# A two-layer graph attention kernel: nodes taken in 25 groups that fit 17 slots of edges, in place of blocks of 128 nodes with 18 slots

## The chip, the cores and the metric

The kernel runs on one core of a Trainium2 chip. The metric is the device time of one execution in microseconds (us). Engines are named as in the profile: PE is TensorE's matmul and PEld its weight load, DVE is VectorE, ACT is ScalarE, POOL is GpSimd and SP is SyncE.

## The reference

There are 3125 nodes with 768 features each, and 53125 edges that are sorted by destination. An edge has a source, a destination and one of three types. Two relational graph attention layers run one after the other (four heads in the first, one in the second); then the input is added and each row is normalized.

```python
def rgat_conv(x, W, q, k, b, src, dst, etype, heads, out_ch, n_nodes):
    xr = jnp.einsum('nd,rdf->rnf', x, W)
    oi = xr[etype, dst]
    oj = xr[etype, src]
    alpha = jax.nn.leaky_relu(oi @ q + oj @ k, NEG_SLOPE)
    m = jax.ops.segment_max(alpha, dst, num_segments=n_nodes)
    e = jnp.exp(alpha - m[dst])
    z = jax.ops.segment_sum(e, dst, num_segments=n_nodes)
    a = e / (z[dst] + EPS)
    msg = (a[:, :, None] * oj.reshape(-1, heads, out_ch)).reshape(-1, heads * out_ch)
    return jax.ops.segment_sum(msg, dst, num_segments=n_nodes) + b

h = jax.nn.elu(rgat_conv(x, W1, q1, k1, b1, src, dst, edge_type, 4, 192, n))
x = _layernorm(x + rgat_conv(h, W2, q2, k2, b2, src, dst, edge_type, 1, 768, n), axis=-1)
```

The number of edges that end in a node is not constant: it is drawn, 17 on average.

## The kernel before

Edges are handled in **slots** of 128, one edge to a partition. Nodes are handled in 25 **blocks** of 128 (the last has 53). The edges of a block lie in one run of the sorted list, whose start is counted on the chip and read by SP into a register. A block always takes `SL = 18` slots, 2304 edges, from its start on; the last block takes `SLL = 9`. Edges behind the block's own are in the window too, and `a_index2` gives them an index out of bounds, so that the gather leaves them out. All in all there are `NK = 24 * 18 + 9 = 441` slots, and each slot is gone through three times. Were a block to have more edges than its slots hold, a flag would be set and a second, general kernel would run behind this one.

Every engine's instructions stand in an order that is written out by hand: each of the three phases has a table of events, `ev`, by step, and the recording loop goes through the steps.

- **The prelude** (`prepare`, `weights_kq`, `nodes_kq`) loads W and x, makes the small table of source scores `kt1` (four numbers for each node and type) and the destination scores `qq`, and writes four lists of edges to HBM (`ed_d`, `dr_d`). In `prepare` a loop of 26 DVE instructions (L205) counts the edges below each block's border; a matmul sums these counts over partitions into `starts`. The pieces of `prepare` are spread between the other work by `more(n)`.
- **Phase 1** (`phase1`) has 144 steps with one `d_group` each: 18 matmuls (L629) that make one half row block of the table `tab1`, the rows x W. `d_row` copies it out on ACT (L641) and SP stores it. Six steps make one block of nodes, and beside them the attention weights of one block are worked out: SP loads the lists (`a_load` L471, `a_load2` L477, `a_window` L511), `a_index` turns them on PE (L516), `a_index2` makes the indices, `a_gathers` gathers 18 x 128 source scores with one indirect DMA for each slot from POOL's queue (L451, `kt`), `a_q` to `a_q3` add the destination's score, `a_alpha` (L565) adds the two and is the instruction that waits for the gathers, and `a_max`, `a_scan`, `a_back`, `a_put` make the weights `pall`.
- **Phase 2** (`phase2`) gathers whole rows of `tab1`, 3088 bytes for each edge, again one indirect DMA for each slot (L451, `share`, nine buffers). ACT weighs them (`high`, L788), DVE makes the remainder (`low`, L802), POOL or DVE makes the selecting matrix (`sel`, L790: POOL for two slots of three) and four matmuls sum a slot into its node rows (`sums`, L821). The last block goes first (`order`), then blocks 0 to 23. When a block is summed, `e_y` to `e_s2` make its hidden rows, and 18 pieces of six matmuls (`d_part`, L876), one with each slot of the next block, make its rows of `tab2`; `d_row` (L884) copies them and SP stores them (L890).
- **Phase 3** (`phase3`) gathers rows of `tab2` in the same way (L451, `G`, a ring of 36 slots as six tiles of six). `a_alpha` (L1013) waits for all gathers of a block; `a_turn`, `a_scan` (with the list that L966 loads), `a_exp`, `a_back`, `a_put` make the weights, `high` and `low` the parts, `sums` (L1090) the sums. `LAG = SL + 11` steps lie between a slot's gather and its sum. `e_y` to `e_out` normalize a block and store it.

POOL's gathers of all phases stand in one queue, `gather_rows` is the helper that issues them, so all have the line L451 and are told apart by the tile they fill: `kt`, `share`, `G`.

Of the kernel before, what the change touches and what calls it, by code (L numbers as in the profile page):

```python
# [37 lines left out]
SL = 18  # L38
CAP = SL * P

SLL = 9

FRONT = 256
BACK = CAP + 256

PART = 6
# [5 lines left out]
def kernel(  # L52
# [8 lines left out]
):  # L61

# [26 lines left out]
    NK = (NB - 1) * SL + SLL  # L89
# [5 lines left out]
    first_rows = {0: 0, 1: 1, 2: 2, NB - 1: 3}  # L95
# [4 lines left out]
    tab2 = dram.tile([NP * R, RW], F32, name="ftab2")  # L100
    kt1 = dram.tile([NP * R, 4], F32, name="kt1")
    xb_d = dram.tile([NP, D], F32, name="xb_d")
# [11 lines left out]
    starts = keep.tile([1, 32], I32, name="starts")  # L114
# [3 lines left out]
    dl = keep.tile([P, NB, SL], F32, name="fdl")  # L118
    rel = keep.tile([P, NB, SL], F32, name="rel")
    pall = keep.tile([P, NB, SL, H1], F32, name="pall")  # L120
    q1s = keep.tile([P, NB, H1, R, 3], BF, name="q1s")
# [48 lines left out]
    def prepare(work, bank, wide, half):  # L170
# [7 lines left out]
        cnt = work.tile([EP, 32], F32, name="cnt")  # L178
        V.memset(cnt, 0.0)
# [20 lines left out]
        blk = tile_(I32)  # L200
        V.tensor_single_scalar(blk, di, 7, op=ALU.logical_shift_right)
        bb, junk, dr = (half[:EP, i * ET:(i + 1) * ET] for i in range(3))
        V.tensor_copy(bb, blk)
        for b in range(NB + 1):
            V.tensor_scalar(junk, bb, float(b), 0.0, op0=ALU.is_lt, op1=ALU.add, accum_out=cnt[:, b:b + 1])  # L205
            yield
            if b == 10:
                win = wide[:EP, :ET + P]
                c = ed_d[1:2, FRONT:FRONT + 1]
                G.dma_start(win, bass.AP(tensor=c.tensor, offset=c.offset, ap=[[ET, EP], [1, ET + P]]))  # L210
                rx = tile_(F32)
                V.scalar_tensor_tensor(rx, si, float(R), ti, op0=ALU.mult, op1=ALU.add)
                store(ed_d[0], rx)
                yield
                tf = tile_(F32)
                V.tensor_copy(tf, ti)
                store(ed_d[2], tf)
                yield
                V.tensor_single_scalar(di, di, P - 1, op=ALU.bitwise_and)
                V.tensor_copy(dr, di)  # L220
                store(dr_d[0], dr)
                yield
# [3 lines left out]
        V.tensor_reduce(cnt[:, 30:31], junk, AX.X, ALU.add)  # L226
        yield
        V.tensor_tensor(junk, dB, win[:, P:ET + P], op=ALU.is_equal)
        V.tensor_reduce(cnt[:, 31:32], junk, AX.X, ALU.add)
# [8 lines left out]
        T.matmul(pc[:1, :32], ones, cnt, start=True, stop=True)  # L238
        cf = work.tile([1, 32], F32, name="cf")
        V.tensor_copy(cf, pc[:1, :32])  # L240
        V.tensor_copy(starts, cf)
        yield
        big = work.tile([1, 32], F32, name="big")
        V.tensor_sub(big[:, :NB], cf[:, 1:NB + 1], cf[:, 0:NB])
        V.tensor_scalar(big[:, :NB - 1], big[:, :NB - 1], float(CAP), None, op0=ALU.is_gt)
        V.tensor_scalar(big[:, NB - 1:NB], big[:, NB - 1:NB], float(SLL * P), None, op0=ALU.is_gt)
        V.tensor_copy(big[:, 30:32], cf[:, 30:32])
        V.memset(big[:, NB:30], 0.0)
        tot = work.tile([1, 1], F32, name="tot")
        V.tensor_reduce(tot, big, AX.X, ALU.add)  # L250
        V.tensor_copy(flag, tot)
# [90 lines left out]
    def nodes_kq(buf, pre, work, psum, bank, wk, kqs, wH, wL, qq, more, edges_ready):  # L342
# [86 lines left out]
        for m in range(1, NCH + 2):  # L429
# [7 lines left out]
            more(3)  # L437
# [5 lines left out]
    ends = {min((b + 1) * SL, NK) - 1 for b in range(NB)}  # L443
# [10 lines left out]
    def start(b, into):  # L454
        if b not in into:
            into[b] = nc.sync.value_load(starts[0:1, b:b + 1], min_val=0, max_val=E)
        return into[b]

    def at(t, rw, off, ap, s):

        c = t[rw:rw + 1, bass.ds(s + (FRONT + off), 1)]
# [36 lines left out]
    def phase1(pre, work, psum, wH, wL, qq):  # L498
        kts = [work.tile([P, SL, H1], F32, name=f"kt{i}", bufs=1) for i in range(3)]
        als = [work.tile([P, SL + 2, H1], F32, name=f"al{i}", bufs=1) for i in range(2)]  # L500
        for t in als:
            V.memset(t, 0.0)
# [165 lines left out]
        def slots(b):  # L668
            return SLL if b == NB - 1 else SL

# [1073 lines left out]
```

## Time and profile before

| what | value |
|---|---|
| runs before | 2519.32 us median of 3 (2488.62, 2519.32, 2528.63) |
| profiled execution, its own time | 2285.11 us |
| its span, first to last instruction | 2283.3 us |
| mean granted TensorE clock in it | 0.950 |
| PE busy | 2049.8 us (90%), 11055 matmuls |
| DVE busy | 1555.7 us (68%) |
| ACT busy | 1401.7 us (61%) |
| POOL busy | 1733.3 us (76%), 1685 instructions |
| gathers of POOL | 3 x 441 |
| moved by DMA | 508.22 MB |

The profiled execution is one run with the profiler on. Busy times count what an engine executes, not the gaps in which it issues; a PE that is busy is not PE at its peak, since the ends of matmuls are modelled. [...]

### The profile page before, as it was taken

Reading aid. Unit: us, or ns where it says so; the run is one execution under the profiler, and the core shown is the slowest. Engines: PE = TensorE matmul, PEld = TensorE weight load, DVE = VectorE, ACT = ScalarE, POOL = GpSimd, SP = SyncE. Lnnn points to the kernel's source line nnn. Section 1 sums busy time; section 2 is a strip of 40 time slices with the busy share of each in tenths; the row PEclk is TensorE's granted clock in tenths of the full one; section 3 lists DMA queues with packets and bytes.
Section 4 is the critical chain, followed back from the end, with each engine's and each line's share of the span. In section 5 each row is a group of like instructions: output and inputs, shape, how many; then the busy total and the mean of one; then the engine's idle time right before and its main releaser. Section 6 shows DMA issues by size and latency. Waiting matters only on the chain.

```text
span 2283.3 us, 37563 instructions
## 1 busy us (share of the span) xinstructions
PE 2049.8 (90%) x11055; PEld 1765.0 (77%) x11055; DVE 1555.7 (68%) x4075; ACT 1401.7 (61%) x3197; POOL 1733.3 (76%) x1685
## 2 busy tenths in 40 slices
PE   6998988898886899999999999999489999899986
PEld 5888888888886799999999999999255555565554
DVE  7734434343432899999999999996266666676666
ACT  5411111111111788888888888885278888787885
POOL 4267777777776888888888888884677777777772
PEclk9989998999998899999999999999699999999998
DMA  6554544454455877777777777776788888888881
GB/s 181 178 149 164 170 145 145 161 170 145 159 184 158 308 245 234 233 230 235 234 235 237 228 233 240 236 233 219 256 283 298 298 306 299 288 273 281 278 289 65
DMA packets 153595, 508.22 MB, mean 223 GB/s; under 512 B 40404, under 2 KB 53723, under 8 KB 153383
## 3 DMA queue, kind: packets, MB, share of 16 engines
q0 software_dynamic: 85472, 334.19, 48.2%
q1 hardware_dynamic: 57681, 155.56, 19.0%
q10 hardware_dynamic: 10230, 15.98, 2.2%
q8 instruction: 91, 1.49, 0.3%
q14 instruction: 121, 0.99, 0.1%
HBM read 428.40 MB, written 94.04 MB: 229 GB/s over the span
## 4 chain that ended last, share of the span: by engine, by line
PE 38%; POOL 7%; DMA 6%; issue 6%; DVE 6%; ACT 4%; POOLq 0%; DVEq 0%; ACTq 0%
PE po L876 14%; PE acc L821 11%; PE acc L1090 10%; DMA G<-ftab,ridx 5%; POOL share L451 3%; POOL sel L790 2%; DVE L L802 2%; POOL G L451 1%; ACT H L1068 1%; DVE L L1079 1%; PE pt L851 1%; DMA G<-ftab,rfirst 1%; DMA share<-ftab,ridx 1%; PE pa L1020 0%; PE bc L977 0%
## 5 line engine op out<-in xcount | busy, mean ns | idle before, releaser
L788 ACT ACTIVATE H<-share,pall 128x193 fp32r<-128x193 f32 x1748 | 642.7, 447 | 104.9 <-DMA share<-ftab,ridx 36.6
L802 DVE SCALAR_TENSOR_TENSOR L<-share,pall,H 128x193 fp32r<-128x193 f32 x1748 | 648.6, 437 | 25.2 <-ACT H L788 17.7
L876 PE MATMUL po<-wH,hT 128*128 128x386 f32 (+1 forms) x1800 | 532.8, 339 | 0.0
L451 POOL DMA_INDIRECT G<-ftab,ridx x378 | 421.9, 1116 | 115.2 <-issue 58.8
L451 POOL DMA_INDIRECT kt<-kt,ridx x378 | 405.2, 1072 | 115.1 <-issue 113.9
L451 POOL DMA_INDIRECT share<-ftab,ridx x378 | 428.1, 1133 | 81.3 <-DVE L L802 42.0
L629 PE MATMUL po<-wH,xT 128*128 128x384 f32 x1584 | 444.1, 353 | 0.7 <-ACT xT L615 0.7
L1090 PE MATMUL acc<-G,selp 128*128 128x386 f32 x904 | 357.0, 521 | 0.3 <-ACT selp L1064 0.3
L876 PEld LDWEIGHTS po<-wH,hT 128*128 128x128 f32 x1800 | 334.4, 189 | 0.6 <-DVE hT L864 0.5
L876 PE MATMUL po<-wL,hT 128*128 128x386 f32 (+1 forms) x900 | 304.7, 339 | 0.0
L629 PEld LDWEIGHTS po<-wH,xT 128*128 128x128 f32 x1584 | 301.3, 196 | 3.4 <-issue 0.8
L641 ACT COPY share<-po 128x384 f32<-128x384 f32 x144 | 68.9, 479 | 337.0 <-PE po L629 267.2
L629 PE MATMUL po<-wL,xT 128*128 128x384 f32 x792 | 274.7, 347 | 0.0
L821 PE MATMUL acc<-H,sel 128*128 128x386 f32 x874 | 242.5, 359 | 20.6 <-POOL sel L790 10.9
L1079 DVE SCALAR_TENSOR_TENSOR L<-G,p,H 128x772 fp32r<-128x772 f32 x215 | 218.9, 1020 | 59.9 <-ACT H L1068 59.5
L1090 PEld LDWEIGHTS acc<-G,selp 128*128 128x128 f32 x904 | 171.6, 201 | 84.1 <-issue 19.9
L790 POOL TENSOR_SCALAR sel<-frow,fdl 128x128 fp32r<-128x128 f32 x291 | 226.1, 777 | 13.0 <-PE acc L821 1.1
L821 PE MATMUL acc<-L,sel 128*128 128x386 f32 x874 | 227.0, 341 | 0.0
L1068 ACT ACTIVATE H<-G,p 128x772 fp32r<-128x772 f32 x215 | 199.1, 928 | 3.9 <-DVE p L1044 3.8
L821 PEld LDWEIGHTS acc<-H,sel 128*128 128x128 f32 x874 | 149.6, 190 | 55.2 <-POOL sel L790 46.2
L565 DVE TENSOR_TENSOR a<-qe,kt 128x72 f32<-128x72 f32 x25 | 5.8, 233 | 242.8 <-DMA kt<-kt,ridx 213.3
L876 PEld LDWEIGHTS po<-wL,hT 128*128 128x128 f32 x900 | 169.6, 188 | 0.0
(231 smaller groups left out, 3009.7 us busy)
## 6 DMA issues: line engine op xcount, KB each, us to landing
ftab<-r SPq DMA_DIRECT2D x75, 386.0 KB
ftab<-share SPq DMA_DIRECT2D x72, 386.0 KB
sT<-dr_d SPq DMA_DIRECT2D x25, 576.0 KB
share<-in_L_gnn_W_dram SPq DMA_DIRECT2D x36, 384.0 KB
w_d<-w2hl SPq DMA_DIRECT2D x18, 768.0 KB
share<-in_x_dram SPq DMA_DIRECT2D x25, 384.0 KB
xb_d<-share SPq DMA_DIRECT2D x25, 384.0 KB
xr<-in_x_dram SPq DMA_DIRECT2D x23, 384.0 KB
```

Of the source, the lines that this page charges most:

```text
L451: G.indirect_dma_start(out=to, out_offset=None, in_=tab, in_offset=_index(i[:, j:j + 1]), bounds_check=NP * R - 1, oob_is_err=False)
L629: T.matmul(po[:, :HALF], xT[:, s, t, :], w[:, i, sl], start=(n == 0), stop=(n == 3 * DT - 1))
L641: S.copy(to, po[:, :HALF].rearrange("p (h f) -> p h f", h=2))
L788: S.activation(H[:, c], g[:, c], AF.Copy, scale=pall[:, b, j, h:h + 1])
L790: (V if k % 3 == 0 else G).tensor_scalar(sel, row, dl[:, b, j:j + 1], None, op0=ALU.is_equal)
L802: V.scalar_tensor_tensor(L[:, c], g[:, c], pall[:, b, j, h:h + 1], H[:, c].bitcast(F32), op0=ALU.mult, op1=ALU.subtract)
L821: T.matmul(acc[:, c, :HW], sel, a[:, c * HW:(c + 1) * HW], start=(j == 0 and i == 0), stop=(k in ends2 and i == 1), skip_group_check=True)
L851: T.transpose(pt[:, t // 3, (t % 3) * P:(t % 3 + 1) * P], s["ey"][:, t * P:(t + 1) * P], ident)
L876: T.matmul(po[:, :wd], hT[:, k, t, :], w[:, r * DT + t, sl], start=(t == 0 and n == 0), stop=(t == DT - 1 and n == 2))
L1068: S.activation(H, g, AF.Copy, scale=p)
L1079: V.scalar_tensor_tensor(L, g, blk[b]["p"][:, j:j + 1], st[k][1].bitcast(F32), op0=ALU.mult, op1=ALU.subtract)
L1090: T.matmul(acc[:, c, :HW], sel, a[:, c * HW:(c + 1) * HW], start=(j == 0 and i == 0), stop=(k in ends and i == len(parts) - 1))
```

## The change

A group of nodes is no longer 128 nodes by number. It is as many whole nodes, 128 at most, as fit 17 slots of edges (14 in the first group); the next group begins with the node that did not fit. The number of groups stays at 25, and `NK` is `24 * 17 + 14 = 422`. Where a group begins is known only when the group before it has been read: `a_next` and `a_next2` work it out from that group's list, with two small matmuls that spread a number over the partitions, and write both starts, of edges and of nodes, to `starts`. SP reads them before it loads the next group's list. The counting loop in `prepare` is gone. The dense part of phase 1 still goes by blocks of 128 nodes.

Rows that belonged to a block by its number now lie at an address that is read at run time: the destination scores go through HBM (`q1_d`), rows of `tab2` are stored at the group's start and the next group's store goes over the rows that were not this group's own, and the output is stored in the same way. The last group's output is scattered by an indirect DMA from POOL. Phase 2 goes through the groups in order, from the first. Phase 3's ring is one tile of 36 slots.

```diff
-SL = 18
+SL = 17
-SLL = 9
+SLF = 14
...
-    NK = (NB - 1) * SL + SLL
+    NK = (NB - 1) * SL + SLF
...
-        for b in range(NB + 1):
-            V.tensor_scalar(junk, bb, float(b), 0.0, op0=ALU.is_lt, op1=ALU.add, accum_out=cnt[:, b:b + 1])
-            yield
...
     def start(b, into):
+        if b == 0:
+            return 0
         if b not in into:
-            into[b] = nc.sync.value_load(starts[0:1, b:b + 1], min_val=0, max_val=E)
+            into[b] = nc.sync.value_load(starts[0:1, 0, b:b + 1], min_val=0, max_val=E)
         return into[b]
+
+    def nodes(b, t):
+        if b == 0:
+            return t[0:P]
+        return t[bass.ds(nc.sync.value_load(starts[0:1, 1, b:b + 1], min_val=0, max_val=N), P)]
...
     def a_load2(work, b):
...
+        s["q"] = work.tile([P, H1 * R * 3], BF, name="q1", bufs=2)
+        nc.sync.dma_start(s["q"], nodes(b, q1_d))
...
+        def a_next(b):
+            s = st[b]
+            pT = s["pi"]
+            T.matmul(pT[:, 64:65], ident[0:1, 0:1].to_broadcast([1, P]), dl[0:1, b, slots(b):slots(b) + 1],
+                     start=True, stop=True)
+            n, m = (n_all[:, b + c:b + c + 1] for c in (0, 1))
+            V.tensor_scalar(m, pT[:, 64:65], n, s["lim"], op0=ALU.add, op1=ALU.min)
+            own = work.tile([P, 1], F32, name="own", bufs=2)
+            V.tensor_sub(own, m, n)
+            s["cnt"] = work.tile([P, 1], F32, name="cnt", bufs=2)
+            junk = work.tile([P, SL], F32, name="inv", bufs=2)
+            V.tensor_scalar(junk, dl[:, b, :SL], own, 0.0, op0=ALU.is_lt, op1=ALU.add, accum_out=s["cnt"])
+
+        def a_next2(b):
+            s = st[b]
+            pT = s["pi"]
+            T.matmul(pT[:, 66:67], rel3[:, 1, 0:1].to_broadcast([P, P]), s["cnt"], start=True, stop=True)
+            c, m = (slice(b + i, b + i + 1) for i in (0, 1))
+            V.tensor_scalar(s_all[:, m], pT[:, 66:67], s_all[:, c], float(E), op0=ALU.add, op1=ALU.min)
+            V.tensor_copy(starts[0:1, 0, m], s_all[0:1, m])
+            V.tensor_copy(starts[0:1, 1, m], n_all[0:1, m])
...
-        steps = ((-9, a_loads), (-9, a_loads2), (-6, a_index), (-5, a_index2), (-5, a_gathers), (1, a_q), (2, a_q2),
+        chain = ((-6, a_index), (-6, a_index2), (-5, a_gathers), (-5, a_next), (-4, a_next2))
+        for b in range(1, NB):
+            for d, f in chain:
+                ev.setdefault(6 * b + d + (b == 1), []).append((f, b))
+        steps = ((-10, a_loads), (-9, a_loads2), (1, a_q), (2, a_q2),
                  (2, a_window), (3, a_q3), (4, a_alpha), (5, a_max), (6, a_scan), (7, a_back), (8, a_put))
-        last = ((-14, a_loads), (-9, a_loads2), (-9, a_index), (-8, a_index2), (-8, a_gathers), (-4, a_q), (-3, a_q2),
-                (-3, a_window), (-2, a_q3), (-1, a_alpha), (0, a_max), (1, a_scan), (2, a_back), (3, a_put))
...
-        order = [NB - 1, *range(NB - 1)]
+        order = range(NB)
...
-            for m in range(SL):
+            for m in range(6 * R):
                 rc = divmod(m // 3, 2)
-                k = e + m if i else first + 2 + m * (SL + 5) // SL
+                k = e + m * SL // (6 * R) if i else first + 2 + m * (SL + 6) // (6 * R)
...
-                nc.sync.dma_start(
-                    tab2[b * P * R:(b + 1) * P * R, :].rearrange("(p r) f -> p r f", r=R)[:, r, :], o)
+                nc.sync.dma_start(nodes(b, tab2.rearrange("(n r) f -> n r f", r=R))[:, r, :], o)
...
-        gs = [work.tile([P, PART, RW], F32, name=f"G{i}", bufs=1) for i in range(NT)]
+        gs = work.tile([P, NG, RW], F32, name="G", bufs=1)
...
-            nc.sync.dma_start(out[b * P:b * P + n, :], y[:n])
+            if b == NB - 1:
+                i = G.indirect_dma_start(out=out, out_offset=_index(oidx), in_=y, in_offset=None, bounds_check=N - 1,
+                                         oob_is_err=False)
+            elif b == 0:
+                i = nc.sync.dma_start(out[0:P, :], y)
+            else:
+                n = nc.sync.value_load(starts[0:1, 2, b:b + 1], min_val=0, max_val=N - P)
+                i = nc.sync.dma_start(out[bass.ds(n, P), :], y)
```

## The prediction

> **What bounds the kernel now.** I read the busy table of the page first, then POOL's timeline in each phase, because a share of busy time hides the gaps in which an engine issues.
>
> ```profile
> span 2283.3 us, 37563 instructions
> PE 2049.8 (90%) x11055; PEld 1765.0 (77%) x11055; DVE 1555.7 (68%) x4075; ACT 1401.7 (61%) x3197; POOL 1733.3 (76%) x1685
> ```
>
> PE looks like the bound and POOL like an engine with a quarter of its time to spare. POOL's timeline in phase 1 says otherwise (start, duration, line, the idle time before it):
>
> ```profile
> 127.19 0.99 POOL L451 DMA_INDIRECT kt<-kt,rfirst  x1 [0.30 <-issue]
> 128.49 1.03 POOL L451 DMA_INDIRECT kt<-kt,rfirst  x1 [0.31 <-issue]
> ...
> 727.68 1.00 POOL L451 DMA_INDIRECT kt<-kt,rfirst  x1 [0.30 <-issue]
> ```
>
> Every gather follows the one before it by 1.30 us, 1.00 of work and 0.30 of issue, with no wait between. From the first (124.46) to the last (727.68) that is 603.2 us for 440 steps, 1.371 each. So **phase 1 is POOL's queue**. DVE's waits there name the victim, `a_alpha`:
>
> ```profile
> DVE a L565 <- DMA kt<-kt,ridx: 202.9, 21, 15.2
> ```
>
> PE is next. The windows (columns PE, PEld, DVE, ACT, POOL, clock, DMA share, GB/s) of phases 1, 2 and 3:
>
> ```profile
> 124.00:729.00 605.00, 531.65 (x3298) 509.90 (x3298) 237.24 (x513) 106.35 (x208) 470.19 (x441) 0.95 0.50 163
> 801.00:1548.00 747.00, 737.89 (x4081) 704.12 (x4081) 718.70 (x2090) 653.07 (x1760) 651.09 (x659) 1.00 0.78 234
> 1608.00:2233.00 625.00, 545.66 (x2320) 337.96 (x2321) 396.55 (x915) 483.84 (x871) 490.10 (x441) 0.92 0.87 289
> ```
>
> In phase 1 PE works 531.65 / 24 = 22.2 us per block against POOL's 18 x 1.371 = 24.7.
>
> In **phase 3** POOL again goes gather after gather, first at 1608.82, last at 2232.13: 623.3 / 440 = 1.417 us each. The page's row `L451 POOL DMA_INDIRECT G` lists waits, but POOL's timeline shows only gaps of 0.30 us, the issue itself. DMA is busy 87%.
>
> In **phase 2** PE (98.8%), DVE (96%) and POOL are all close. POOL's timeline shows three slots, as two of three have their `sel` on POOL:
>
> ```profile
> 1128.43 1.09 POOL L451 DMA_INDIRECT share<-ftab,ridx  x1 [0.17 <-DVE L L802]
> 1129.56 0.81 POOL L790 TENSOR_SCALAR sel<-frow,fdl 128x128 fp32r<-128x128 f32 x1
> 1130.54 1.09 POOL L451 DMA_INDIRECT share<-ftab,ridx  x1 [0.17 <-DVE L L802]
> 1131.93 1.21 POOL L451 DMA_INDIRECT share<-ftab,ridx  x1 [0.30 <-issue]
> 1133.17 0.63 POOL L790 TENSOR_SCALAR sel<-frow,fdl 128x128 fp32r<-128x128 f32 x1
> 1133.98 1.08 POOL L451 DMA_INDIRECT share<-ftab,ridx  x1 [0.18 <-issue]
> ```
>
> From 1128.43 to 1133.98 it is never idle longer than an issue: 5.55 us, 1.85 per slot, 33.3 per block. ACT's `ey` rows (L839, one per block) stand at 801.10 and 1548.08 with 22 blocks between: 33.95 each. When the gathers have run out, the last block takes 31.62 (1548.08 to 1579.70), and that is PE alone: 120 matmuls of `d_part` run in 21.17 us by the chain, 0.176 each, so 180 of them are 31.8. So POOL sets phase 2's pace too, and PE follows 2 us per block behind.
>
> **Part 1, fewer slots in phase 1.** 441 gathers become 422: 19 x 1.371 = **-26.0 us** (24.7 at the bare 1.30). It holds if the next engine is faster: POOL's group becomes 17 x 1.371 = 23.3, PE's 22.2 and what is added. Added on PE are two one-column matmuls per group (nearest row L516, 0.27 us): +0.5; one `pq` matmul of 0.034 us goes. PE: 22.7 against 23.3. It holds by 0.6 us per group, so what is late next is PE. Ends: 0 and -26; I take -25.
>
> **Part 2, the chain of starts.** A group's list can be loaded only after the group before it has been read. DVE gets some eleven instructions of 0.16 to 0.20 us per group (rows L522, L525, L1112), about 2 us; it waits about 9.7 us per block for `kt`, so they are hidden. SP gets one or two register loads per group; its instructions beside such loads take 0.03 to 0.05 us and `T`'s own issue 0.83. The order puts the load (step 6b-10) four steps before its use (6b-6). A step is 24.7 / 6 = 4.1 us, so 16 us are there for a load that is otherwise awaited nowhere. Behind the register load on SP stand stores of `tab1` rows and the `sT` and `q1` loads: they have row buffers and whole steps to spare. Nothing is behind it on POOL: the indices of group b are made while POOL still issues those of b-1. Cost 0; the other end is rival B.
>
> **Part 3, the windows.** [...] `a_window` has 18 rows against 72 partitions now, [...] By the trace the load has four steps, 16 us, until `a_scan`, and DVE's waits never name it. [...]
>
> **Part 4, prelude.** The counting loop goes: 26 x (0.591 + 0.082) = 17.5 us of DVE. DVE is busy 36.6 of the 40 us from 20 to 60, then PE is. About half of the loop lay there, and the other pieces of `prepare` move into it: ends 0 and -8, I take **-3**. `q1_d`, written in pieces of 72 bytes, delays PE's first `pq` matmuls by some us; POOL has 14 gathers, 19 us, to issue meanwhile: 0.
>
> **Part 5, from phase 1 to 2.** Now POOL stands still for 9.2 us after its last `kt` gather:
>
> ```profile
> 728.68 8.28 issue
> 737.88 4.72 DMA share<-ftab,rfirst
> ```
>
> The first `share` gather needs the last store of `tab1`, whose copy on ACT stands behind `e` (L586), which needs the last `kt` gathers. In the new order that copy stands before the last group's `e`, 17 gathers earlier. The wait goes; late next is the last group's own chain (731.21 to 737.81 now) that stands ahead of `high` on ACT. First sum about 8.5 us after the last `kt` gather in place of 15.2: -6.7. But the first group has 14 slots, not 9, before `d_part` starts: five slots at 1.9 (steady pace), up to 2.6 (743.84 to 770.2 for ten slots): +9.5. Together **+3**, ends -3 and +7.
>
> **Part 6, phase 2.** After `d_part` has begun 407 slots are left in place of 431, 24 fewer. If PE set the pace alone each would save 4 x 0.176 = 0.71 us: -17. If POOL does, 33.95 / 18 = 1.89: -45. A group would take POOL 32.1 and PE 30.9 to 31.7, so POOL still leads, narrowly; I take 32.3 per group, 1.65 less: **-40**. The stores of `tab2` now each wait for the one before (overlapping rows); they are 11 us apart, and behind a waiting store on SP stand only more stores, with three row buffers: 0.
>
> **Part 7, phase 3.** 19 x 1.417 = -26.9; at the bare 1.31, -24.9. [...] **-26**. Bytes stay, 87% of 625 = 544 us of DMA, under the 598 that POOL needs. PE, ACT and DVE have 545.66, 483.84 and 396.55 and shrink with the slots. The tail loses one of 29 steps (40 us): -1.4, and the last output's scatter costs an indirect DMA's issue and landing: +2; each output store now waits for the one before, a group (some 24 us) earlier: 0. Together **+1**.
>
> **The sum**: -3 -25 +3 -40 -26 +1 = **-90 us** on 2285.1, so 2195, a ratio of 0.961. The timed runs lie higher, 2519.3 at the median and 2488.6 at the lowest; no view says where those 234 us are. Spread evenly they make 2420; as a constant 2429. I take **2430**.
>
> **Rival A, PE is the bound in the timed runs.** If the 234 us are PE's, 24 x (22.2/c - 24.7) + 25 x (31.6/c - 34.0) = 234 at c = 0.79 of full pace. For it: the page's clock row has slices below 9, and the runs scatter by 1.6%. Against it: POOL needs no clock to be late. Then phase 1 loses 24 x 0.6 = 15, phase 2 gains 24 x 0.71/0.79 = 21, start and tail cost 4, phase 3 gives 26 (POOL still): -28, **2491**, no change.
>
> **Rival B, the chain starves POOL, slower.** Place: the first gather of each group. Price: whatever `T` is late, 24 times. It decides when load, two matmul rounds and the register loads, queued on SP behind a store that waits for DVE (longest wait on SP there 12.8 us), come more than a group's 23.3 us after the group before; at 5 us too late per group, 120 - 90: **2549**. Against it: half a group of slack by the order.
>
> **Rival C, DMA rules phase 3**: denser slots, same bytes, no gain there: 2456.
>
> **Rival D, the groups don't fit** and the general kernel runs behind. Cutting the drawn edges by the rule gives 104 nodes first and 108 in the last of 25: it fits.
>
> **Chances.** Main course 0.62, A 0.22, B 0.08, C 0.07, D 0.01. The measurement tells about 2% from no change, 50 us: faster 0.66, within 0.25, slower 0.09. Main course alone 2390 to 2465; the range to 2500 takes in A and C.
>
> **What would show it.** `kt` gathers from first to last in about 578 us, with gaps of 0.30 between groups too: a longer gap at a group's first gather is B. `a_alpha`'s wait at about 8 us per group. `ey` rows 32.3 us apart: 33.2 means PE. G gathers in about 598 us. No idle POOL between `kt` and `share`. A gain under 40 us or a DVE wait for `w` or `f` would prove me wrong.

## The result, and the profile after

The changed kernel takes 2546.16 us at the median (14 runs, 2531.52 to 2561.24) and the kernel before, on the same chip, 2521.12 us (14 runs, 2488.62 to 2543.30): a ratio of **1.013**, 95% interval 1.009 to 1.017. Forecast were 2430 us, 0.965 of the runs before (0.961 on the profiled execution). The profiled execution of the changed kernel took 2544.64 us, so unlike that of the kernel before it is an ordinary one. This matters: the experiments below show that the same two kernels gave 0.954 on another chip of the same type.

The page, first lines and the clock row (tenths of full speed in 40 slices of the span):

```profile
span 2542.9 us, 37652 instructions
...
PE 2146.1 (84%) x10953; PEld 1811.9 (71%) x10953; DVE 1530.3 (60%) x4159; ACT 1358.3 (53%) x3095; POOL 1670.1 (66%) x1615
...
PEclk9977778787888777899999999999959999999898
```

The clock is low in slices 3 to 14, which is phase 1, and nearly full behind it. The windows of phases 1, 2 and 3 (PE, PEld, DVE, ACT, POOL busy, clock, DMA share, GB/s) say the same:

```profile
122.00:985.00 863.00, 661.77 (x3311) 573.13 (x3311) 269.73 (x776) 101.38 (x205) 441.46 (x422) 0.79 0.36 114
1038.00:1754.00 716.00, 705.38 (x3976) 691.45 (x3976) 684.67 (x1999) 625.47 (x1682) 625.35 (x626) 1.00 0.80 246
1848.00:2496.00 648.00, 528.41 (x2199) 319.43 (x2200) 380.03 (x854) 463.86 (x834) 472.13 (x422) 0.90 0.84 278
```

From first to last `kt` gather phase 1 takes 863 us, where 603 were before and 578 were forecast. POOL works for 441 of them. Its timeline at the border of two groups, and its waits in phase 1 (in total, times, longest):

```profile
448.90 1.00 POOL L461 DMA_INDIRECT kt<-kt,ridx  x1 [0.30 <-issue]
461.43 1.00 POOL L461 DMA_INDIRECT kt<-kt,ridx  x1 [11.53 <-DVE lim L554]
462.73 1.00 POOL L461 DMA_INDIRECT kt<-kt,ridx  x1 [0.30 <-issue]
```

```profile
POOL kt L461 <- DVE lim L554: 286.1, 22, 21.6
```

`lim` (L554) is the last of DVE's instructions that make a group's indices. A gap at a group's first gather is what the prediction named as the sign of rival B, the chain of starts. It isn't that chain. One group's list `T` was issued at 469.4 (its packets in the trace land by 471.1), but the transpose on PE that makes indices of it ran over 25 us later, since it stands in PE's queue behind the row groups of four steps; over all groups the median of this distance is 25.6 us, and 13.5 us on the chip of e7 below:

```profile
L490 SPq DMA_DIRECT2D T<-ed_d x1: 687/687/687, 469.4 to 469.4; - x1
L538 PE MATMUL pT<-fident,T x1: 262/262/262, 496.0 to 496.0; 54*128 54x54 f32 x1
```

So **PE is late, and POOL is its victim**. How PE is late stands in the timeline and in the windows of one group. The timeline first, from where the stretch begins (the rows of SPq are SP's issues):

```profile
470.83 1.57 POOL L461 DMA_INDIRECT kt<-kt,ridx  x1 [0.31 <-issue]
...
471.64 0.01 SPq L532 DMA_DIRECT2D w<-ed_d  x1
471.69 0.34 PE L694 MATMUL po<-wH,xT 128*128 128x384 f32 x1 [0.51 <-issue]
472.38 0.00 SPq L734 DMA_DIRECT2D w_d<-w2hl  x1
472.42 0.19 PEld L694 LDWEIGHTS po<-wH,xT 128*128 128x128 f32 x1 [1.38 <-issue]
...
473.12 0.00 SPq L708 DMA_DIRECT2D ftab<-share  x1
473.13 0.34 PE L694 MATMUL po<-wH,xT 128*128 128x384 f32 x1 [1.10 <-issue]
```

```profile
460.00:466.00 6.00, 6.00 (x35) 5.49 (x34) 4.17 (x14) 1.89 (x4) 3.66 (x4) 1.00 0.20 68
471.60:477.00 5.40, 3.02 (x11) 2.18 (x11) 0.00 (x0) 0.00 (x0) 4.18 (x5) 0.83 0.62 227
477.00:483.00 6.00, 3.99 (x10) 2.49 (x9) 2.19 (x5) 0.00 (x0) 4.61 (x5) 0.50 0.40 107
483.00:486.60 3.60, 1.69 (x6) 0.96 (x5) 0.00 (x0) 0.51 (x2) 1.00 (x1) 0.50 0.03 1
486.60:492.00 5.40, 5.37 (x17) 5.38 (x18) 1.82 (x2) 1.06 (x2) 0.00 (x0) 0.50 0.48 169
```

Up to 471 PE is fully busy and starts a matmul every 0.17 us. Then, for some 15 us, many of its instructions, matmuls and weight loads alike, come 0.72 us apart (471.69, 472.42, 473.13); the releaser is "issue", which means that PE waited for nothing that the profile shows. I call this the stutter. SP's instructions come at the same spacing (471.64, 472.38, 473.12). ACT and DVE wait for PE's results; POOL goes on with its gathers. Behind the stutter TensorE's clock is halved: 0.50 until 492, though PE is 99% busy again in the last row. Narrower windows show where it changes:

```profile
471.78:475.19 3.41, 1.73 (x7) 1.17 (x7) 0.00 (x0) 0.00 (x0) 2.62 (x3) 1.00 0.81 315
488.85:492.25 3.40, 3.40 (x13) 3.40 (x12) 0.66 (x1) 0.00 (x0) 0.00 (x0) 0.50 0.54 175
492.30:496.00 3.70, 3.70 (x24) 3.39 (x22) 0.00 (x0) 0.48 (x1) 0.00 (x0) 1.00 0.38 153
```

The clock drops at 475.2 and is full again from 492.3. In the 3.41 us before the drop PE was busy for 1.73; in the 3.40 us before the return, at the half clock, for all of them. The half clock comes behind the stutter, which began 3.5 us before the drop (471.7). So it is in most places: of the 30 times that the clock drops to 0.50 in this window of phase 1 (122 to 985), 25 come 1.9 to 4.9 us behind the beginning of a stretch of stutter, counted as under "What stays open". That the stutter lowers the clock is my reading of this order; what lowers it is not shown, and in the profile of before it drops 13 times in phase 1 without one such stretch.

### The profile page after: what moved, and what is told of

Same layout as the page of the kernel before. It is cut to its first block, busy times and chain, and to the rows that moved or that the text cites. A ratio compares the mean times of both kernels' runs of the same rounds, so it can differ in the third digit from the quotient of the medians.

```text
span 2542.9 us, 37652 instructions
## 1 busy us (share of the span) xinstructions
PE 2146.1 (84%) x10953; PEld 1811.9 (71%) x10953; DVE 1530.3 (60%) x4159; ACT 1358.3 (53%) x3095; POOL 1670.1 (66%) x1615
## 4 chain that ended last, share of the span: by engine, by line
PE 58%; issue 7%; another core or an unknown queue 7%; DVE 4%; ACT 3%; POOL 2%; DMA 2%; ACTq 0%; SPq 0%; POOLq 0%; DVEq 0%
PE po L942 17%; PE acc L1161 14%; PE po L694 13%; PE acc L887 11%; PE bc L1043 1%; POOL share L461 1%; DVE L L868 1%; DVE L L1150 1%; PE pt L917 1%; ACT H L1139 1%; POOL sel L856 1%; PE px L673 1%; ACT sT L1049 0%; POOL G L461 0%
## 5 line engine op out<-in xcount | busy, mean ns | idle before, releaser
L854 ACT ACTIVATE H<-share,pall 128x193 fp32r<-128x193 f32 x1672 | 620.0, 450 | 97.8 <-PE acc L887 35.1
L461 POOL DMA_INDIRECT kt<-kt,ridx x374 | 393.9, 1053 | 392.1 <-DVE lim L554 270.7
L868 DVE SCALAR_TENSOR_TENSOR L<-share,pall,H 128x193 fp32r<-128x193 f32 x1672 | 620.2, 437 | 21.6 <-issue 15.6
L694 PE MATMUL po<-wH,xT 128*128 128x384 f32 x1584 | 506.1, 386 | 103.7 <-issue 81.3
L694 PEld LDWEIGHTS po<-wH,xT 128*128 128x128 f32 x1584 | 334.1, 216 | 136.4 <-issue 105.5
L1161 PE MATMUL acc<-G,selp 128*128 128x386 f32 x868 | 345.5, 524 | 9.2 <-ACT selp L1134 6.6
L694 PE MATMUL po<-wL,xT 128*128 128x384 f32 x792 | 299.8, 379 | 33.1 <-issue 32.8
L1150 DVE SCALAR_TENSOR_TENSOR L<-G,p,H 128x772 fp32r<-128x772 f32 x205 | 208.3, 1018 | 87.8 <-ACT H L1139 55.8
L887 PE MATMUL acc<-H,sel 128*128 128x386 f32 x836 | 226.6, 353 | 12.8 <-POOL sel L856 11.1
L694 PEld LDWEIGHTS po<-wL,xT 128*128 128x128 f32 x792 | 171.9, 217 | 51.1 <-issue 51.0
L1139 ACT ACTIVATE H<-G,p 128x772 fp32r<-128x772 f32 x205 | 190.2, 929 | 10.1 <-remote 7.8
L1161 PE MATMUL acc<-H,sel 128*128 128x386 f32 x410 | 149.9, 447 | 27.5 <-DVE sel L1141 17.9
```

The lines of the kernel that those rows point to most:

```text
L461: G.indirect_dma_start(out=to, out_offset=None, in_=tab, in_offset=_index(i[:, j:j + 1]), bounds_check=NP * R - 1, oob_is_err=False)
L694: T.matmul(po[:, :HALF], xT[:, s, t, :], w[:, i, sl], start=(n == 0), stop=(n == 3 * DT - 1))
L854: S.activation(H[:, c], g[:, c], AF.Copy, scale=pall[:, b, j, h:h + 1])
L868: V.scalar_tensor_tensor(L[:, c], g[:, c], pall[:, b, j, h:h + 1], H[:, c].bitcast(F32), op0=ALU.mult, op1=ALU.subtract)
L887: T.matmul(acc[:, c, :HW], sel, a[:, c * HW:(c + 1) * HW], start=(j == 0 and i == 0), stop=(k in ends2 and i == 1), skip_group_check=True)
L1139: S.activation(H, g, AF.Copy, scale=p)
```

## Experiments

They ran in seven sets on different chips of the same type; the kernels of one set share a chip. This is needed to read them, for the kernel before itself takes 2290 to 2299 us on chips 2 and 14 (the "short sets" of the expectations) and 2487 to 2526 us on chips 4, 5, 7 and 13, as on the chip of the result ("long sets"). The profiled execution of the kernel before, 2285 us, on which the prediction's sums were made, fits only the first kind. Chip 13 was long in both of its sets; each other chip was seen in one set, so a trait of the chip and one of the hour are not told apart.

| kernel | chip | us | ratio to the kernel before, 95% | first to last `kt` |
|---|---|---|---|---|
| before, e1 | 2 | 2291 (one) | | 603.2 |
| window 18, e2 | 2 | 2194 | 0.955 (0.951 to 0.958) | 575.4 |
| before, window 17, e3 | 2 | 2300 | 1.000 (0.999 to 1.002) | 603.4 |
| q1 on chip, e4 | 2 | 2201 | 0.959 (0.955 to 0.962) | 575.0 |
| changed, e5 | 5 | 2549 | 1.009 (1.007 to 1.012) | 862.9 |
| before, e6 | 14 | 2289 | 1.000 | 602.5 |
| changed, e7 | 14 | 2188 | **0.954** (0.945 to 0.963) | 571.3 |
| window 18, e8 | 14 | 2185 | 0.952 (0.945 to 0.959) | 572.2 |
| q1 on chip, e9 | 14 | 2186 | 0.953 (0.946 to 0.960) | 573.8 |
| before, e10 | 4 | 2490 (one) | | 745.3 |
| static starts, e11 | 4 | 2443 | 0.985 (0.970 to 1.000) | 773.7 |
| window 18 and q1, e12 | 4 | 2473 | 0.994 (0.991 to 0.997) | 804.6 |
| changed, e13 | 13 | 2496 | **1.001** (0.996 to 1.005) | 828.5 |
| loads on ACT, e14 | 13 | 2457 | 0.986 (0.981 to 0.991) | 783.6 |
| window 18, e15 | 13 | 2458 | 0.986 (0.982 to 0.990) | 792.1 |
| window 18 and ACT, e16 | 13 | 2515 | 1.012 (1.005 to 1.019) | 846.7 |
| before, loads on ACT, e17 | 13 | 2500 | 1.009 (1.005 to 1.013) | 770.8 |
| PE shifted, e18 | 7 | 2545 | 1.011 (1.003 to 1.019) | 868.5 |

### First set: the window load of 17 rows or q1's load?

From the result's profile I suspected the load that the prediction's Part 3 had put at 0, the window load, which has 17 rows of 4 where it had 18, and took the chain or q1's load for rivals. e1 is the kernel before as it is.

> The kernel before, unchanged, to see where an ordinary execution of it (2521 us at the median) spends the 234 us by which the execution profiled so far (2285 us) was shorter. Theory 1 (phase 1 of the ordinary execution is slow as well, its TensorE clock half gated as in the changed kernel): first to last kt gather takes 800 us or more in place of 603, clock in that stretch about 0.8 in place of 0.95, phases 2 and 3 as before. Theory 2 (spread over all phases): each phase is about 10% longer. If the profile falls again on a 2285 us execution, only the list of times and clocks tells something.

It showed only the short kind, as the last sentence had allowed for. e2 gives the window load 18 rows again:

```diff
-s["f"] = work.tile([H1 * SL, 3 * P + 1], F32, name="w", bufs=2)
-nc.sync.dma_start(s["f"], at(ed_d, 3, -P - 1, [[P, SL], [0, H1], [1, 3 * P + 1]], start(b, regs)))
+s["w"] = work.tile([H1 * (SL + 1), 3 * P + 1], F32, name="w", bufs=2)
+nc.sync.dma_start(s["w"], at(ed_d, 3, -P - 1, [[P, SL + 1], [0, H1], [1, 3 * P + 1]], start(b, regs)))
+s["f"] = s["w"][:H1 * SL]
```

> The changed kernel with one row more in the window load of phase 1 (18 rows of 4, 72 partitions, of which 68 are used), nothing else. Theory W ([...] transfers and engines stutter while it lasts): its packets take 1 to 2.5 us in place of 4.9 to 6.3, the kt gathers run from first to last in 580 to 640 us in place of 863, clock in phase 1 back to 0.95, total 2270 to 2350. Theory C (the chain of starts makes phase 1 late): nothing changes, phase 1 stays at 863 and the total at 2546. Theory Q (loading q1 in pieces of 72 bytes does it): the same, no change.

e3 does the reverse to the kernel before:

```diff
-nc.sync.dma_start(s["f"], at(ed_d, 3, -P - 1, [[P, SL], [0, H1], [1, 3 * P + 1]], start(b, regs)))
+n = SL - 1
+for i, c in ((0, n), (n, 1)):
+    nc.sync.dma_start(s["f"][i * H1:(i + c) * H1],
+                      at(ed_d, 3, i * P - P - 1, [[P, c], [0, H1], [1, 3 * P + 1]], start(b, regs)))
```

> The kernel before, in which the window load of phase 1 is cut into 17 rows of 4 and 1 row of 4[...]; nothing else. Theory W: phase 1 takes 800 us or more from first to last kt gather, with PE and SP stuttering after each of these loads, and the total is 2500 to 2600; if ordinary executions of the kernel before already have a slow phase 1, little is added to those. Theories C and Q: phase 1 as in the kernel before.

e4 takes q1 from SBUF by block number, so it computes with the wrong nodes:

```diff
-s["q"] = work.tile([P, H1 * R * 3], BF, name="q1", bufs=2)
-nc.sync.dma_start(s["q"], nodes(b, q1_d))
...
-                         s["q"], start=True, stop=True)
+                         q1b[b], start=True, stop=True)
...
+        q1b = [q1s[:, b].rearrange("p k s -> p (k s)") for b in range(NB)]
```

> The changed kernel with q1 read from SBUF by block number (so with the wrong nodes for a group), without the load from HBM and without the register load in front of it on SP. Theory Q: the second half of the stutter, from about 8 to 14 us after the window load, goes, phase 1 drops from 863 to about 700 us, total about 2390. Theory W: at most 50 us come off, total 2500 to 2546. Theory C: one register load less per group on SP, total 2500 to 2546 as well.

Read by itself, e2 would have been taken for a proof of theory W: it goes that theory's way, and beyond its numbers (2194 us, where 2270 to 2350 were expected). But e4, which leaves the window alone, gives the same time, and e3 shows that a window load cut into 17 rows and 1 costs the kernel before nothing (1.000). On this chip nothing was slow to begin with. What the set does show is the load itself. By its packets in the trace a window load lasts about 1.1 us at the median in the kernel before, 5.1 us in e3 with 17 rows, and 1.0 us in e8 with 18. In the profile of before up to 12 of its packets of 1540 bytes are under way at once, and one starts every 0.011 us at the median; in the result's profile, with 17 rows, there are never more than 2 at once, one starts every 0.062 us, and a load lasts 5.8 us. Why 17 rows go so is not shown. e3's time shows that the longer load costs nothing here.

### Second set: the changed kernel as it is

> The changed kernel, unedited. In the four runs before this one the kernel before took 2299 us in its ordinary executions and the changed kernel with one of two edits 2194 and 2201, so either both edits take away the same slow phase 1, or the slow phase 1 belongs to the executions measured first and not to the change. Theory W or Q (a property of the changed kernel): 2500 to 2560 us, kt gathers over about 863 us, clock in phase 1 about 0.79. Theory D (a disturbance that came with the first set of executions, of both kernels): 2190 to 2205 us, kt gathers over 575 us with gaps of 0.30, ratio to the kernel before 0.953 to 0.96.

Theory W's and Q's number, but with the kernel before at 2526 us beside it. Between this set and the last, kernels and chip had both changed, so neither W nor D was decided: the anchors belong in the same set as the edits.

### Third set: a short one with its anchors

> The kernel before, unedited. The kernel before has taken 2525 us in one set of executions and 2299 us in another, so there are two kinds of set, and all four kernels of this set share one. In a long set (before at about 2525 us) this shows for the first time where its 226 us are; theory P (the long set slows phase 1 of every kernel): kt gathers over about 800 us, phases 2 and 3 longer by 5 to 25 us together. In a short set: 603 us, as known.

> The changed kernel, unedited, in the same set. Short set, theory D (the slow phase 1 comes with the set and not with the change): 2190 to 2205 us, kt gathers over 575 us, ratio 0.955. Short set, theory W or Q: about 2540 us, ratio 1.1. Long set: 2548 us and 863 us again.

> The changed kernel with 18 rows in the window load of phase 1, in the same set. Long set, theory W [...]: at least 100 us less than the changed kernel. Long set, theory Q or C: within 30 us of the changed kernel. Short set: within 10 us of the changed kernel by each.

> The changed kernel with q1 read from SBUF by block number (wrong nodes for a group), without its load and the register load for it, in the same set. Long set, theory Q: at least 100 us less than the changed kernel. Theory W: within 50 us of it. Short set: within 10 us of it by each.

Theory D: the slow phase 1 comes with the chip. Here the changed kernel gains 4.6%, and window and q1 edits change nothing: theory D holds. POOL's timeline of e7, at the first gathers and where phase 1 goes over into phase 2, and its waits there:

```profile
127.37 1.11 POOL L461 DMA_INDIRECT kt<-kt,rfirst  x1 [21.48 <-DVE own L565]
128.78 1.04 POOL L461 DMA_INDIRECT kt<-kt,rfirst  x1 [0.30 <-issue]
...
698.65 1.00 POOL L461 DMA_INDIRECT kt<-kt,ridx  x1 [0.30 <-DMA ftab<-share]
699.95 1.00 POOL L461 DMA_INDIRECT share<-ftab,rfirst  x1 [0.30 <-issue]
```

```profile
POOL kt L461 <- DVE lim L554: 0.5, 1, 0.5
```

The wait for the new indices, 286.1 us in the result's profile, is 0.5 us here, and POOL goes from the last `kt` gather to the first `share` gather without a pause. The windows of e7's three phases:

```profile
127.00:699.00 572.00, 533.69 (x3379) 511.87 (x3379) 276.23 (x796) 105.47 (x210) 443.19 (x422) 0.97 0.56 174
735.00:1485.00 750.00, 737.41 (x4162) 723.55 (x4161) 716.41 (x2091) 655.60 (x1758) 655.42 (x654) 1.00 0.79 245
1545.00:2151.00 606.00, 528.27 (x2238) 325.99 (x2237) 386.06 (x869) 470.67 (x850) 477.49 (x422) 0.92 0.88 297
```

PE has the same work in phase 1, at clock 0.97 in place of 0.79, and takes 533.69 us busy in place of 661.77.

### Fourth set: a long one; where the kernel before loses its time, and the chain

> The kernel before, unedited, for a look at where a long set of executions (about 2525 us) has its 226 us more than a short one (about 2295). Theory P (phases 1 and 3 of a long set are hit, each block after its loads on SP, phase 2 is not): kt gathers over 750 to 820 us in place of 603, phase 2 within 10 us of 828, G gathers 640 to 660 us, TensorE's clock in phase 1 about 0.82. In a short set: 603, 828, 630, as known.

This is the profile that the prediction lacked. Theory P holds, with the `kt` gathers (745 us) just under its 750 to 820. These are the windows of its three phases, and its page's rows for `po` on PE and for the `kt` gathers (the last column is the idle time before them and what ended most of it):

```profile
122.00:868.00 746.00, 570.67 (x3132) 522.51 (x3130) 229.89 (x495) 100.89 (x198) 467.19 (x441) 0.84 0.38 123
921.00:1680.00 759.00, 740.72 (x4083) 705.83 (x4082) 725.52 (x2109) 660.29 (x1779) 661.86 (x667) 1.00 0.78 239
1775.00:2433.00 658.00, 545.77 (x2276) 330.69 (x2276) 390.21 (x897) 475.90 (x855) 491.63 (x441) 0.91 0.83 274
```

```profile
L629 PE MATMUL po<-wH,xT 128*128 128x384 f32 x1584 | 484.1, 376 | 127.9 <-issue 83.5
L451 POOL DMA_INDIRECT kt<-kt,ridx x378 | 402.1, 1064 | 252.0 <-DVE rel L526 142.9
```

In e6, the short set, the first of these rows has 0.4 us of idle time, in this one 127.9:

```profile
L629 PE MATMUL po<-wH,xT 128*128 128x384 f32 x1584 | 443.2, 352 | 0.4 <-issue 0.2
```

So on such a chip the kernel before, too, is bound by PE in phase 1, and its POOL, too, waits for indices (143 us) that it never waited for in the profile of before. Phase 2 takes what it took.

e11 writes the starts in as constants for these inputs:

```diff
-        if b not in into:
-            into[b] = nc.sync.value_load(starts[0:1, 0, b:b + 1], min_val=0, max_val=E)
-        return into[b]
+        return EDGE0[b]
...
-        return t[bass.ds(nc.sync.value_load(starts[0:1, 1, b:b + 1], min_val=0, max_val=N), P)]
+        return t[NODE0[b]:NODE0[b] + P]
```

> The changed kernel with every group's first edge and first node written in as constants for these inputs: no register loads from the chain of starts, no wait of SP for DVE in front of T, sT, q1, the rows of tab2 and xb; everything else as it was. Short set: within 10 us of 2188 (the chain costs nothing, Part 2 of the prediction). Long set, theory C (the chain, or the loads by register, is what a long set punishes in the changed kernel): at least 80 us under 2548. Long set, theories W and Q: within 30 us of 2548.

e12 joins the edits of e2 and e4.

> The changed kernel with both edits: 18 rows in the window load of phase 1, and q1 from SBUF by block number (wrong nodes for a group) without its load. Short set: 2175 to 2195. Long set, theory W or Q: phase 1 down by 100 us or more, total 2380 to 2450. Long set, theory C or none of them: 2500 to 2550.

In microseconds e11 is 105 under the 2548 that its theories name, but the kernel before is 38 us faster on this chip than beside e5. The unedited changed kernel was not in this set, so e11 and e12 are read by their ratios, against 1.001 to 1.013 for it. Against these the constants are worth 1.6 to 2.8%, 40 to 70 us, on a chip of the long kind: short of C's 80, more than W's and Q's 30. These are two runs with an interval of 0.970 to 1.000, so neither is decided, and a gain is likely but not shown. Phase 1 is still 774 us, 28 more than in the kernel before, with 19 gathers fewer. The joint edit gave 0.994, 2473 us, which lies between the numbers of the theories.

### Fifth and sixth set: window, SP or ACT

> The changed kernel, unedited, as the anchor of this set. Long set (before at 2490 to 2525 us): 1.009 to 1.013 of the kernel before, kt gathers about 860 us. Short set (before at about 2295): 0.954, kt gathers 572 us.

e13 came at 1.001 and 828.5 us, below both numbers expected for a long set: what the changed kernel loses differs among these chips too.

e14 moves the loads from SP's queue to ACT's:

```diff
-            into[b] = nc.sync.value_load(starts[0:1, 0, b:b + 1], min_val=0, max_val=E)
+            into[b] = nc.scalar.value_load(starts[0:1, 0, b:b + 1], min_val=0, max_val=E)
...
-        nc.sync.dma_start(s["T"], at(ed_d, 0, 0, [[LL, 3], [P, SL + 1], [1, P]], r0))
+        nc.scalar.dma_start(s["T"], at(ed_d, 0, 0, [[LL, 3], [P, SL + 1], [1, P]], r0))
...
```

and in the same way the loads of `sT`, `q1` (with its register load) and the window; phase 3 reads its starts on SP.

> The changed kernel with the dynamic loads of phase 1 (T, window, sT, q1) and their register loads issued by ACT in place of SP; the stores of rows and the loads of x and W stay on SP. Theory S (in a long set PE is held up in step with SP's instructions, so what SP issues beside PE is what costs): kt gathers under 750 us, total at least 100 us under the changed kernel of this set. Theory L (it is the loads themselves, whoever issues them): within 40 us of the changed kernel. Short set: within 20 us of the changed kernel by both, unless ACT, waiting for the chain of starts, is late with the rows of tab1.

> The changed kernel with 18 rows in the window load of phase 1, in the same set. Long set, theory W: at least 40 us under the changed kernel of this set, kt gathers 800 us or less. If q1's load is what matters of the two (both together gave 0.994 of the kernel before): within 15 us of the changed kernel. Short set: within 10 us.

Each takes 38 us off 2496, in phase 1 (828.5 to 783.6 and 792.1 us). For e14 that is far less than theory S had (100) and inside theory L's 40: its number came. For e15 it is just short of theory W's 40, while its gathers (792 us) meet W's 800; the other course, 15 us, is missed. The timeline of e14 shows PE's stutter while SP has nothing to issue (behind the store at 367.13 SP issues nothing for over 12 us):

```profile
367.13 0.38 SPq L710 DMA_DIRECT2D ftab<-share  x1
...
367.85 0.19 PEld L696 LDWEIGHTS po<-wH,xT 128*128 128x128 f32 x1 [0.92 <-issue]
...
368.57 0.19 PEld L696 LDWEIGHTS po<-wH,xT 128*128 128x128 f32 x1 [0.53 <-issue]
...
369.30 0.19 PEld L696 LDWEIGHTS po<-wL,xT 128*128 128x128 f32 x1 [0.54 <-issue]
```

The steps are 0.72 us again, so PE isn't held up by SP's instructions: **theory S is out**. The row of the `kt` gathers in e13 and in e15, from their pages:

```profile
L461 POOL DMA_INDIRECT kt<-kt,ridx x374 | 393.7, 1053 | 357.9 <-DVE lim L554 237.6
```

```profile
L461 POOL DMA_INDIRECT kt<-kt,ridx x374 | 394.0, 1054 | 322.6 <-DVE lim L555 207.3
```

With the window on 18 rows POOL's idle time falls by 35 us, 30 of them at the indices. Most of it stays.

> The changed kernel with both edits that helped: 18 rows in the window load of phase 1, and T, window, sT and q1 with their register loads issued by ACT. Long set: if the two gains (38 us each on 2496) are separate, 0.970 of the kernel before, about 2420 us, kt gathers about 750 us; if both take away the same stretch of stutter, 0.985, kt gathers about 785. Short set: 0.950 to 0.957, about 2185 us.

> The kernel before with T, window, sT and their register loads issued by ACT in phase 1. Long set, theory S (SP's instructions hold PE up, in both kernels): kt gathers fall from about 745 to under 700 us, total 40 us or more under the kernel before. Theory K (in the kernel before these loads are no cause, since nothing makes them wait): within 15 us of it. Short set: within 10 us of it.

Neither of the two courses of e16 came: together the edits give 1.012, worse than either and no better than none (1.001 in the other set of this chip). e17 is over the kernel before, by 13 us at the median of all runs and by 0.9%, 22 us, by the ratio: at the edge of K's 15 or beyond it; S had it 40 us under. So edits move a long set by 1 to 3%, in a direction that I could not foresee. Of those of these two sets only the window's ran on a short one, where it changes nothing (e8).

### Seventh set: does any edit do it?

e18 adds instructions that nobody needs, once, at the start of phase 1:

```diff
         a_next2(0)
+        for _ in range(64):
+            T.transpose(st[0]["pi"][:, 128:128 + 3 * (SL + 1)], st[0]["T"], ident[:3 * (SL + 1), :3 * (SL + 1)])
```

> The changed kernel with 64 more transposes on PE (128 instructions, written to a part of PSUM that nobody reads) once, at the start of phase 1. Their own price is 4 to 10 us on PE at most. Theory Y (in a long set the stretches of stutter fall where they fall, and any edit shifts them): in a long set the ratio to the kernel before differs by 0.01 or more from that of the changed kernel (1.0006 to 1.013 in three sets), so below 0.99 or above 1.023. Theory N (the edits that gave 0.986 had found parts of the cause): 1.000 to 1.015. Short set: 0.954 to 0.958 by both.

1.011, inside what the changed kernel itself gave: theory N's number, and no support for Y, from one shift on one chip. It does not explain e16.

## Why the prediction was wrong, by its own steps

Two pairs of profiles let each part be held against a number. The short pair is e6 and e7, from one set; the long pair is e10 and e13, from chips 4 and 13, on which the kernel before takes 2488 and 2496 us.

| stretch | forecast | short: before, changed | change | long: before, changed | change |
|---|---|---|---|---|---|
| to the first `kt` gather (Part 4) | -3 | 123.8, 127.4 | +3.6 | 122.3, 123.0 | +0.7 |
| first to last `kt` (Parts 1 to 3) | -25 | 602.5, 571.3 | **-31.2** | 745.3, 828.5 | **+83.2** |
| to the last `share` (Parts 5, 6) | -37 | 834.6, 802.6 | -32.0 | 864.8, 812.1 | -52.7 |
| to the last `G` (Part 7) | -26 | 668.7, 649.3 | -19.4 | 700.5, 678.9 | -21.6 |
| tail (Part 7) | +1 | 51.7, 41.5 | -10.2 | 55.6, 48.7 | -6.9 |
| sum | -90 | 2281.2, 2192.1 | **-89** | 2488.5, 2491.2 | **+3** |

**The step that failed** is the last one of "The sum": "The timed runs lie higher (...); no view says where those 234 us are. Spread evenly they make 2420; as a constant 2429." Neither is so. Between e6 and e10, the kernel before on a chip of either kind, 207 us lie: 143 in phase 1, 25 between the last `kt` and the first `share` gather, 5 in phase 2, 32 in phase 3 and 2 at the ends. Those in phase 1 change what phase 1 is bound by. A tenth of the time was put down to a factor, when it stood for an execution of another kind than the one that had been profiled.

**Part 1** fell with it. Its condition was "It holds if the next engine is faster", with 0.6 us per group to spare. In its place the long pair shows PE as the bound of phase 1: -25 us were forecast there, +83 came (+3 in all, where -90 were forecast). On a chip of the short kind PE was faster and the part gave 31 us, more than the 25. On the long kind PE takes 31 us per block in the kernel before (745.3 / 24) and 34.5 per group after it, against the 23.8 that POOL needs (571.3 / 24), and 19 gathers fewer are worth nothing.

**Rival A** had the right place, PE, and the wrong price. It slowed PE by one factor in phases 1 and 2; in e10 and e13 phase 2 has a clock of 1.00 and its parts gave all that they give elsewhere. And it had 15 us for the loss of phase 1, where 83 came. In windows of that phase, PE's busy time goes from 570.67 (of 746) to 633.45 us (of 829) for nearly the same matmuls and its idle time from 175 to 196; on the short kind both kernels have about 530 busy. So the changed kernel loses more time in both ways. The window of e13:

```profile
123.00:952.00 829.00, 633.45 (x3314) 559.08 (x3315) 269.51 (x778) 101.08 (x205) 442.05 (x422) 0.83 0.38 119
```

**Rival B** named the sign, a gap at the first gather, with another cause: T had lain there for 25 us. Its chain may bear on a long set (e11), but not by a late list: in e13, too, `T` is issued 24.7 us (median) before it is turned.

**Part 2**, the chain at no cost: right on the short kind, where POOL's wait for the indices is 0.5 us. On the long kind static starts (e11) may be worth about 2% against the changed kernel on other chips, which no part had. **Part 3**, the windows, priced at 0 since DVE's waits never named them: the load takes about 6 us at the median by its packets in e7, and 0 was right for the short kind (0.954 with 17 rows, 0.952 with 18). On the long kind, where PE sets the pace, e15 takes 36 us off the `kt` gathers of e13, 1.5 for each of 24 groups; e16, with the same edit, has no gain.

**Part 4** was off by 7 us: the first gather comes later, not earlier. **Part 5** was right: the first sum comes 10.1 us after the last `kt` gather in e7 and 16.3 in e6, -6.2 where -6.7 was forecast, and the first `ey` 36.4 and 34.0 us after it, +2.4 where +3 was. **Part 6** was too high: ACT's `ey` rows in e6 and e7

```profile
L839 ACT ACTIVATE ey<-y x25: 827/847/852, 760.2 to 1574.1; 128x768 f32<-128x768 f32 x25
L905 ACT ACTIVATE ey<-y x25: 830/847/855, 735.1 to 1515.7; 128x768 f32<-128x768 f32 x25
```

take 813.9 and 780.6 us from first to last, -33 where -40 was forecast. In e7 they are 780.6 / 24 = 32.5 us apart, where 32.3 were forecast and 33.2 would have meant PE; in the result's profile they run from 1038.2 to 1819.0, 32.5 as well. **Part 7**: gathers of `G` from first to last in 605.5 us (e7) and 597.3 (e9), where 598 were forecast; the choice of -26 between its two figures was my estimate. Rival C priced phase 3 at no gain; it gained 19 to 22 us. The tail gave 11 us more than thought; the cause is open.

So by parts the sum holds to 1 us where its premise holds, with errors of up to 11 us that cancel, so that the 1 us is in part luck. The time forecast failed for a premise about which execution was being changed.

**What stays open.** Why PE stutters on these chips at all, and why the changed kernel stutters more. PE bound alone, by rival A's own terms, would leave phase 1 at about 745 + 15 = 760 us; 828 to 863 were measured. Window, starts and queue each give some of that back alone (e15, e11, e14), window and queue together give nothing (e16), so they are not separate causes that add up, and no single one is shown. One shift of PE's instructions changed nothing (e18).

The traces do show where the stutter begins. Count as a stretch three or more instructions of PE (weight loads among them), each starting 0.45 us or more after the one before it, with at most 2 us from one to the next. Phase 1 of the result's profile has 36 such stretches, 278 us in all; 33 of them begin within 3 us behind the issue of `T` or `sT`, times that make up 17% of phase 1. In e13 it is 26 of 33, in e18 30 of 33. None of the 36 begins within 3 us behind a load of instructions (queue q8 of the page), and phase 1 of e7, with as many of these loads, has no stretch at all. In e11 none of 19 begins behind `T` (11 in e13), and in e12, where q1's load behind `sT` is gone, one of 22 begins behind `sT` (15 in e13). So what SP does before `T` (register loads, waits) and q1's load are what one would take away together; no run did, and each of these counts is from one trace, e11's and e12's from another chip than e13's. In the kernel before only 5 of 15 stretches of e10 begin behind `T` or `sT`, so this is at most what the change adds.

Of the versions that compute the right result, the changed kernel with 18 rows in the window load is the only one that ran on chips of both kinds and was ahead of the kernel before each time (0.955, 0.952, 0.986, the last clear of noise but under 2%). It was ahead of the changed kernel by 38 us in the one set of the long kind in which both ran.

## What to carry to other kernels

When the profiled execution is 10% shorter than the timed runs, it is not a profile of what is timed: the forecast then needs a case in which the difference sits in one stage and changes its bound, and an experiment needs its anchors on the same chip. An engine with 0.6 us to spare per group is no cover; the saving that stands on it is worth nothing on a chip on which that engine is late. A wait of POOL for an instruction of DVE is to be followed on to the engine whose queue holds the work up: here a transpose that stood behind PE's long matmuls, 25 us after its data had come.

## What the runs showed of the hardware that I had not expected

Chips of one type differ by 8 to 10% on the kernel before, with every execution of it on its chip's side (2276 to 2314 us on chips 2 and 14, 2452 to 2545 on 4, 5, 7 and 13). Most of the difference, 143 of 207 us between e6 and e10, sits in phase 1, where PE on the long chips starts many instructions 0.72 us apart, for some 15 us at 471 in the result's profile, with no wait in the profile. Most stretches of it in the changed kernel begin behind the issue of a group's lists, but load on the DMA engines is not what holds it: from 483.0 to 486.6 in the window above they are 3% busy and move 1 GB/s, and PE still stutters. Phase 2, in which PE is 99% busy and the DMA engines 80%, has none of it. The stutter itself leaves PE idle for 6.3 us in the three rows from 471.6 to 486.6. The clock of 0.50 that follows, from 475.2 to 492.3 here, costs as well: 17 matmuls keep PE busy for 5.37 us in the last row, where 35 took 6.00 us at full clock in the first.
